# Two chunks of one layer a step in place of one chunk of each layer, in a four-layer convolution kernel

## Chip, cores, metric

The kernel runs on one core of a Trainium2 chip, as one program. The metric is device time in microseconds (us) of that core. The engines are TensorE (PE: matrix products; its weight loads are PEld), VectorE (DVE), ScalarE (ACT), GpSimd (POOL) and SyncE (SP, which here only issues DMA transfers).

## What is computed

The input `x` has 16 images of 64 channels of 128 x 128 values in float32. Four layers follow one another, each of the form "x plus a function of the group-normalized x":

```
x = x + L0(gn(x))     # 64x64 gram matrix of the image, applied to it, then a 1x1 product with conv_w
x = x + L1(gn(x))     # per channel two 3x3 gradient filters, |gx| + |gy|
x = x + L2(gn(x))     # a quarter of the channels shifted left, a quarter right, then 3x3 conv W, plus b
x = x + L3(gn(x))     # 3x3 conv w_bin, 1x1 conv w1x1, plus b1x1, batch norm over ALL images, leaky, clip(0, 255)
```

Every normalization needs sums over a whole image before the first value of the next layer can be made. The batch norm in layer 3 needs sums over all 16 images, so the last addition can only be made when layer 3's products of every image are done.

## The kernel before

An image is cut into `NS` = 8 chunks. Each image passes three stages: `Front` (layers 0 and 1, lines 557 to 703), `Layer2` (836 to 994) and `Layer3` (997 to 1086). After all images a tail reads back `x3` (the output of layer 2) and `y` (the convolution of layer 3) from DRAM, or makes `y` again for the six images in `AGAIN`, and writes the output (1334 to 1357).

The order of the work is written out by hand. The class `InOrder` (64 to 76) keeps every engine's instructions in the order in which the program issues them; it is also why the profile shows nearly everything at L74. The main loop (1176 to 1241) goes through steps, and each step has four quarters `q` = 0 to 3. `starts` (1091) says that the front begins at step 15, layer 2 at step 25 and layer 3 at step 35, each 8 steps later for the next image. So a step in the middle handles one chunk of `Front` of image b+2 or so, one chunk of `Layer2` of an earlier image and one chunk of `Layer3` of a still earlier one.

What the stages do in a step, with the names that the profile shows:

- `Front`: TensorE mixes the image with a 64 x 64 matrix (`po<-x,abd`; for images from `EARLY` = 3 on in four 64 x 64 tiles of the array, `mix_four`). ScalarE normalizes the result into `xh`. VectorE makes the two filters in eight instructions (`u`, `e`; method `sobel`, 664): two in quarter 0, four in quarter 1, one in quarter 2 (`u<-xh,co,u`) and one in quarter 3 (`u<-e,co,u`). Ahead of the last two ScalarE takes absolute values of `u` and `e` ("first of 2", 682). The result is stored to DRAM (`x_d<-u`), and ScalarE squares it for the statistics (`junk<-u`).
- `Layer2`: loads a chunk of the front's output (`v<-x_d`), ScalarE normalizes it (`v<-v,co`, `edges`, two single columns `v<-v,kc`, 931 to 949), VectorE makes a difference of neighbouring rows (`d2a`, `d2b`; method `different`, 873), and POOL copies these differences to the other half of the partitions (`q`). TensorE forms `one` (products that two output rows share) and `two` (those that they don't). ScalarE evicts `one` to `c`; VectorE adds `two` and `c` to `x` (908 to 921), and ScalarE squares that (`junk<-x`).
- `Layer3`: the same from tiles in SBUF, with `d` for the difference, and `y` for the sum (1065 to 1087).

Products that use only half of the rows of the array are issued in lists `straight` and `across`; `section` (747) runs them side by side in four quadrants of the array. In steps where both layers have a chunk, layer 3's go to `straight` and layer 2's, from the copy `q`, to `across`. In the other steps (`both_layers` is false, 741) the layers use packed weights (`packed`, 255) and copies of both kinds instead. PSUM has two buffers for `two` and one for `one`.

Before a layer can begin an image, the coefficients must be made: a chain of small instructions (`coefficients`, 300), given out link by link over following quarters by `tick`. TensorE sums (`bank<-st`), VectorE makes mean and variance (`me`, `nv`), POOL takes the power (`va`, `co`). The chains of the Gram matrix (`gram_chain`, 322) go the same way. The Gram products themselves (`bank<-xw`, 128 products of 64 x 65 for an image) lie in three steps of eight; ScalarE copies the rows of the image for them (`xw<-xr`). The first six images have their Gram at double pace (`2 * EARLY`).

All loads and stores of the main loop are issued by SP, except the copies `q` on POOL.

Of the kernel before, what the change touches and what calls it, by code (L numbers as in the profile page):

```python
# [16 lines left out]
P = 128  # L17
# [3 lines left out]
R = 8  # L21
NS = HH // R
EARLY = 3
# [87 lines left out]
def tile_kernel(ctx: ExitStack, tc: tile.TileContext, x, cw_h, w2_t, b2, wbin_t, w1_t, b1, gamma, beta, consts, out):  # L111
# [40 lines left out]
    def planes(d, shift=0):  # L152

        return d[W + shift:W + shift + 2 * C * PLANE].rearrange("(p j w) -> p j w", j=NP, w=W)
# [44 lines left out]
    wb = ring.tile([P, (R + 1) * W + 2], F32, tag="v2", name="wb", bufs=3)  # L199
    wb = wb[0:C, 0:9 * C].rearrange("p (y x c) -> p y x c", y=3, x=3)  # L200
    w1 = ring.tile([P, R + 2, W], F32, tag="v3", name="w1")[0:C, 0, 0:C]
# [23 lines left out]
    d2, q2, d3 = [], None, None  # L225
    for name in ("d2a", "d2b", "q2", "d3"):
        t = wpool.tile([P, 2, CP, W + 2], F32, name=name)
        pool.memset(t, 0.0)
        if name in ("d2a", "d2b"):
            d2.append(t)  # L230
        elif name == "q2":
            q2 = t
        else:
            d3 = t
# [12 lines left out]
    packed = {}  # L247
    cross = wpool.tile([P, 2, C], F32, name="cross")

    def other_weights():  # L250
        for n in range(2):
            o = 1 - single(TO_SLOTS, n)[0]
            pool.tensor_copy(wm[:, :, cols(o)], w2[:, n, :, cols(o)])

        for name, w, table in (("pk2", w2, TO_SLOTS), ("pk3", w3, TO_PAIRS)):
            dve.tensor_add(w[:, 2], w[:, 0], w[:, 1])
            packed[name] = wpool.tile([P, 2, C], F32, name=name)
            for n in range(2):
                o, i = single(table, n)
                for kx, half in ((1, i), (0, 1 - i)):  # L260
                    pool.tensor_copy(
                        packed[name][half * C:(half + 1) * C, n], w[i * C:(i + 1) * C, n, kx, o * C:(o + 1) * C]
                    )
        for n in range(2):
            o, i = single(TO_SLOTS, n)
            for kx in (1, 2):
                pool.tensor_copy(cross[cols(1 - i), kx - 1], w2[cols(i), n, kx, cols(o)])
# [31 lines left out]

    def coefficients(st, put, back=None):  # L300

        yield
        yield from when(TENSOR)
# [6 lines left out]
        yield from rstd(pm, r, me, GN_EPS, None if back is None else co[:, 2:3])  # L310
# [6 lines left out]
        put(co)  # L317

# [3 lines left out]
    def gram_chain(b, pg):  # L322
# [4 lines left out]
        if b > 2 * EARLY:  # L327
            dve.tensor_reduce(gs, pg.rearrange("p (j c) -> p c j", j=3), axis=AX.X, op=ALU.add)
        else:
            dve.tensor_copy(gs, pg)  # L330
        while b > 2 * EARLY and now[0] < NS * b - 4:
            yield
# [61 lines left out]
        abd = stp.tile([P, P], F32, tag="abd", name=f"abd_{b}", bufs=EARLY + 3)  # L394
# [37 lines left out]
        co = stp.tile([P, 5], F32, tag="co1", name=f"co1_{b}", bufs=EARLY + 3)  # L432
# [22 lines left out]
    def first_gram():  # L455
# [7 lines left out]
        for m in range(NS):  # L463
            t = ring.tile([P, 2, CP, W], F32, tag="x3", name=f"x_first_{m}", bufs=NS + 2)
            t = t.rearrange("p a j w -> p (a j w)")
            for h in range(2):
                sp.dma_start(t[h * C:(h + 1) * C], halves(x[0].rearrange("c h w -> (c h w)"), h, m * R, R))
            src.append(t)
        for m in range(NS + 1):
            if m < NS:  # L470
# [3 lines left out]
                for h, copy in ((0, dve.tensor_copy), (1, act.copy)):  # L474
                    copy(xw[:, m * R:(m + 1) * R, 0:C, h], two[:, :, h * C:(h + 1) * C])
# [14 lines left out]
    class Gram:  # L490
        first, last = 2, NS + 2
# [4 lines left out]
        def at(self, i, q):  # L496
# [7 lines left out]
            if i == 2 and q == 0:  # L504
                for m in range(3):
                    self.load(m)
            m = {11: 0, 13: 1, 15: 2, 19: 3, 21: 4, 23: 5, 27: 6, 31: 7}.get(4 * i + q)
# [5 lines left out]
        def part(self, n):  # L513
# [3 lines left out]
            if self.b <= 2 * EARLY:  # L517
# [17 lines left out]
        def half(self, r):  # L535
# [6 lines left out]
            if self.b > 1 and m is not None:  # L542
# [4 lines left out]
                elif self.b < 2 * EARLY:  # L547
                    live.setdefault((Gram, self.b + 1), Gram(self.b + 1)).load(m + 3 - NS)
# [8 lines left out]
    class Front:  # L557
# [14 lines left out]
        def load(self, i):  # L572
            b = self.b
            t = xin.tile([P, R, W], F32, tag="x", name=f"x_{b}_{i}")
            if self.four:
# [3 lines left out]
                for g in range(2):  # L579
                    j = (i * R + g * CP) * W  # L580
                    sp.dma_start(t[cols(g)].rearrange("p h r w -> p h (r w)"), v[:, :, j:j + CP * W])
            else:
                for h in range(2):
                    sp.dma_start(flat(t[h * C:(h + 1) * C]), halves(x[b].rearrange("c h w -> (c h w)"), h, i * R, R))
# [28 lines left out]
        def at(self, i, q):  # L613
            b = self.b
            if q == 0:
# [16 lines left out]
                if i == NS:  # L632
                    chains.append(coefficients(self.st, lambda co: coefs2.update({b: co}), b2_sb))
# [30 lines left out]
        def sobel(self, i, q):  # L664
# [12 lines left out]
            if q == 1:  # L677
                dve.scalar_tensor_tensor(h, h, 3.0, self.u[:, 1:R + 1, :], op0=ALU.mult, op1=ALU.add)
                dve.scalar_tensor_tensor(p, self.e[:, :, 1:W + 2], 3.0, p, op0=ALU.mult, op1=ALU.add)
                dve.tensor_sub(gx, h[:, :, 2:W + 2], gx)  # L680
# [14 lines left out]
        def store(self, i):  # L695
            d = planes(x2_d[self.b]).rearrange("(c s) j w -> c s j w", s=2)
            for h in range(2):
                for s in range(2):
                    j0 = (h * HH + i * R) // 2
                    sp.dma_start(  # L700
                        d[:, s, j0:j0 + R // 2, :],
                        self.x2[i][h * C:(h + 1) * C].rearrange("p (j s) w -> p s j w", s=2)[:, s],
                    )
# [19 lines left out]
    def taps(o, p, wts, srcs, pad=0):  # L723

        made = []
        for kx in (1, 0, 2):
            o0, o1 = (0, W) if kx == 1 else (1, W) if kx == 0 else (0, W - 1)
            for wt, src in zip(wts, srcs):
                made.append((
                    p[cols(o), :, o0:o1], wt[:, kx, cols(o)], src[:, :, o0 + kx - 1 + pad:o1 + kx - 1 + pad]  # L730
# [9 lines left out]

    def both_layers(step):

        return starts[0][1] <= step < starts[1][1] + NS * B
# [31 lines left out]
    def products(p, wts, srcs):  # L775
        issue([taps(o, p, wts, srcs) for o in range(2)])

    def shared(p, wt, t, m=CP):  # L780
        products(p[:, 0:m], [wt], [by_parity(t)[1][:, 0:m]])

    def own(p, n, table, wt, d, pk, q=None, m=CP, both=None):
        d = d[:, n, 0:m]
        o, _ = single(table, n)
        some = [[], []]
        some[1 - o] = taps(1 - o, p[:, 0:m], [wt[:, n] if both is None else both], [d], 1)
        if q is not None:
            some[o] = [
                (p[cols(o), 0:m], pk[:, n], q[:, n, 0:m, 1:1 + W]),  # L790
                (p[cols(o), 0:m, 0:W - 1], wt[:, n, 2, cols(o)], d[:, :, 2:1 + W]),
            ]
        issue(some)

    def apart(two, table, wt, d):

        for kx in range(3):
            for n in range(2):
                o, i = single(table, n)
                straight.append((  # L800
                    two[cols(o), n], wt[cols(i), n, kx, cols(o)], d[cols(i), n, :, kx:kx + W], kx == 0, kx == 2,
                ))

    def apart_across(two, table, q, m):

        for kx in range(3):
            for n in range(2):
                o, i = single(table, n)
                w = W - 1 if kx == 2 else W
                wt = cross[cols(1 - i), kx - 1] if kx else packed["pk2"][cols(1 - i), n]  # L810
                across.append((
                    two[cols(o), n, 0:m, 0:w], wt, q[cols(1 - i), n, 0:m, kx + 1:kx + 1 + w], kx == 0, kx == 2,
                ))
# [22 lines left out]
    class Layer2:  # L836
        first, last = -2, NS

        def __init__(self, b):
            self.b, self.v, self.whole, self.edges, self.p = b, {}, {}, {}, {}  # L840
# [3 lines left out]
        def load(self, i):  # L844
# [4 lines left out]
            t = ring.tile([P, N], F32, tag="v2", name=f"v2_{b}_{i}", bufs=3)  # L849
            for c0, c1, shift in ((0, C // 4, 1), (C // 4, C // 2, -1), (C // 2, C, 0)):  # L850
                cut = R * W + 1 - shift
                parts = [(0, i * R, N)] if i + 1 < NS else [(0, i * R, cut), (cut, -R, N)]
                for at, j, end in parts:
                    for s in range(2):

                        first = j * W + at - 1 + shift
                        src = x2_d[b][W + first:W + first + 2 * C * PLANE].rearrange("(c s n) -> s c n", s=2, n=PLANE)
                        sp.dma_start(t[s * C + c0:s * C + c1, at:end], src[s, c0:c1, 0:end - at])
# [14 lines left out]
        def different(self, i):  # L873

            d, t = d2[i % 2], self.v[i]
            even, odd, _ = by_parity(t)
            difference(d, spread(even, 2 * W), odd, CP if i + 1 < NS else CP - 1)
            for n in range(2):
                _, k = single(TO_SLOTS, n)
                if not both_layers(now[0] + 1):  # L880
                    pool.dma_start(flat(q2[cols(k), n]), flat(d[cols(k), n]))
                pool.dma_start(
                    flat(q2[cols(1 - k), n])[:, 1:CP * (W + 2)], flat(d[cols(k), n])[:, 0:CP * (W + 2) - 1]
                )
# [17 lines left out]
        def at(self, i, q):  # L902
            b = self.b
            closing = i + 1 == NS
            m = CP - 1 if closing else CP
            if q == 0:
                if i == NS:
                    chains.append(coefficients(self.st, self.done))
                if 1 <= i:
                    two = self.p.pop(i - 1)[0]  # L910

                    e = self.edges.pop(i - 1).rearrange("p t (m n) -> p n m t", n=2)
                    ends = two[:, :, :, 0:W:W - 1]
                    dve.tensor_add(ends, ends, e)
                    x3 = ring.tile([P, 2, CP, W], F32, tag="x3", name=f"x3_{b}_{i - 1}", bufs=NS + 2)
                    tiles3[b].append(x3)
                    dve.scalar_tensor_tensor(
                        x3.rearrange("p s j w -> p s (j w)"), two.rearrange("p s j w -> p s (j w)"), 1.0,
                        self.c.unsqueeze(1).to_broadcast([P, 2, CP * W]),
# [476 lines left out]
```

## Time and profile before

Three runs took 2579.61 us in the median (2579.11 to 2585.26). The profiled execution took 2579.28 us, of which its span is 2577.4 us. Its mean granted TensorE clock is 0.974.

| what | value |
|---|---|
| VectorE's first filter instruction of step 15, 24, 25, 35 (start) | 45.22, 145.76, 159.97, 308.57 us |
| the same, step 106, 114 | 1415.89, 1539.73 us |
| the same, step 129, 137, 142 (last) | 1761.87, 1878.66, 1952.19 us |
| last product of layer 3's `two` ends | 2170.7 us |
| DMA in the tail, 2250 to 2450 us | 416 to 417 GB/s |
| DMA over the span | 235 GB/s |
| a copy `q` on POOL: issue, to landing | 0.53 us, 3.0 to 3.3 us |

The start of VectorE's instruction `u<-xh 128x1170` marks a step of the front; there are 128 of them, steps 15 to 142. In a timeline the first number is the start, the second the duration; engines overlap the end of an instruction with the beginning of the next, so what an instruction costs its queue is the distance of two starts. [...]

### The profile page before, as it was taken

Reading aid. Unit: us, or ns where it says so; the run is one execution under the profiler, and the core shown is the slowest. Engines: PE = TensorE matmul, PEld = TensorE weight load, DVE = VectorE, ACT = ScalarE, POOL = GpSimd, SP = SyncE. Lnnn points to the kernel's source line nnn. Section 1 sums busy time; section 2 is a strip of 40 time slices with the busy share of each in tenths; the row PEclk is TensorE's granted clock in tenths of the full one; section 3 lists DMA queues with packets and bytes.
Section 4 is the critical chain, followed back from the end, with each engine's and each line's share of the span. In section 5 each row is a group of like instructions: output and inputs, shape, how many; then the busy total and the mean of one; then the engine's idle time right before and its main releaser. Section 6 shows DMA issues by size and latency. Waiting matters only on the chain.

```text
span 2577.4 us, 52786 instructions
## 1 busy us (share of the span) xinstructions
PE 2436.5 (95%) x19206; PEld 958.9 (37%) x19206; DVE 2091.8 (81%) x2811; ACT 2137.0 (83%) x3549; POOL 504.3 (20%) x805
## 2 busy tenths in 40 slices
PE   6568899999999999999999999999999998999995
PEld 4334343434343434343434343333333333333342
DVE  4998889999999999999999999999997334443433
ACT  4778879898989898989898988888987568877775
POOL 3332312011121212111112121202111100222222
PEclk8778999999999999999999999999999999999998
DMA  8789969898877777777777777778787767999998
GB/s 207 202 230 237 242 171 254 207 251 208 238 188 206 181 199 190 198 190 194 195 182 199 205 188 193 199 201 211 201 201 178 190 197 251 405 417 417 417 413 334
DMA packets 624979, 605.00 MB, mean 235 GB/s; under 512 B 53536, under 2 KB 525504, under 8 KB 624720
## 3 DMA queue, kind: packets, MB, share of 16 engines
q1 hardware_dynamic: 591696, 496.76, 70.0%
q0 software_dynamic: 33024, 104.87, 12.2%
q8 instruction: 153, 2.51, 0.4%
q14 instruction: 106, 0.87, 0.1%
HBM read 321.46 MB, written 243.28 MB: 219 GB/s over the span
## 4 chain that ended last, share of the span: by engine, by line
PE 46%; DMA 20%; DVE 15%; ACT 7%; SPq 7%; issue 4%; POOL 1%; DVEq 0%; POOLq 0%; ACTq 0%
PE two L74 22%; PE one L74 15%; SPq L74 7%; DVE u L74 5%; DMA end_x<-x_d 4%; PE bank L74 3%; DVE e L74 3%; PE po L74 2%; DMA x_d<-u 2%; PE two_again L74 2%; DMA x<-in_x 2%; DMA xw<-x_d 2%; ACT v L74 2%; DVE d L74 2%; DVE y L74 2%
## 5 line engine op out<-in xcount | busy, mean ns | idle before, releaser
L74 PE MATMUL two<-d,w 64*64 64x512 f32 (+2 forms) x2992 | 692.5, 593 | 0.0
L74 PE MATMUL two_again<-v_again,w 64*64 64x508 f32 (+1 forms) x3456 | 374.0, 590 | 10.6 <-ACT v_again L74 10.6
L74 PE MATMUL one<-v,w 128*64 128x508 f32 (+2 forms) x1600 | 362.1, 584 | 7.3 <-ACT c L74 6.9
L74 PEld LDWEIGHTS two<-d,w 64*64 64x64 f32 (+1 forms) x2992 | 206.6, 134 | 418.4 <-issue 408.3
L74 PE MATMUL one<-v,wi 128*64 128x508 f32 (+3 forms) x1536 | 353.7, 595 | 0.0
L74 DVE SCALAR_TENSOR_TENSOR e<-e 128x1032 f32<-128x1032 f32 (+1 forms) x256 | 313.4, 1224 | 0.0
L74 ACT ACTIVATE xh<-po,co 128x128 f32<-128x128 f32 (+1 forms) x480 | 274.7, 622 | 26.7 <-PE po L74 21.4
L74 PE MATMUL po<-x,abd 64*64 64x512 f32 (+1 forms) x1024 | 184.4, 617 | 52.9 <-ACT xh L74 49.7
L74 DVE SCALAR_TENSOR_TENSOR y<-two,c 128x1024 f32<-128x1024 f32 x128 | 156.2, 1220 | 95.1 <-ACT v L74 65.5
L74 PEld LDWEIGHTS two_again<-v_again,w 64*64 64x64 f32 x3456 | 138.4, 134 | 245.4 <-issue 214.4
L74 PE MATMUL two<-q,cross 64*64 64x508 f32 (+3 forms) x944 | 215.9, 573 | 0.0
L74 POOL DMA_DIRECT2D q<-d2b x138 | 72.2, 527 | 721.0 <-DVE d2b L74 417.7
L74 ACT ACTIVATE v<-x,co 128x1024 f32<-128x1024 f32 (+3 forms) x256 | 203.8, 846 | 0.0
L74 POOL DMA_DIRECT2D q<-d2a x138 | 73.8, 537 | 646.3 <-issue 312.7
L74 DVE TENSOR_TENSOR d<-v 128x1024 f32<-128x1024 f32 x128 | 156.3, 1221 | 47.0 <-ACT v L74 29.2
L74 PEld LDWEIGHTS one<-v,w 128*64 128x64 f32 x1600 | 110.9, 137 | 204.2 <-issue 162.9
L74 ACT ACTIVATE v<-v,co 128x1154 f32<-128x1154 f32 x128 | 172.1, 1344 | 14.0 <-DMA v<-x_d 10.4
L74 PE MATMUL two<-d2a,wi 128*64 128x508 f32 (+1 forms) x768 | 183.2, 589 | 0.0
L74 DVE SCALAR_TENSOR_TENSOR u<-xh 128x1170 f32<-128x1170 f32 x128 | 175.9, 1374 | 5.2 <-ACT xh L74 4.4
L74 DVE SCALAR_TENSOR_TENSOR u<-xh,co,u 128x1024 f32<-128x1024 f32 x128 | 163.9, 1280 | 14.6 <-ACT u L74 14.6
L74 PE MATMUL two<-d2b,wi 128*64 128x508 f32 (+3 forms) x768 | 174.3, 565 | 0.0
L74 PEld LDWEIGHTS one<-v,wi 128*64 128x64 f32 x1536 | 101.2, 138 | 193.9 <-issue 156.1
(231 smaller groups left out, 4323.6 us busy)
## 6 DMA issues: line engine op xcount, KB each, us to landing
x<-in_x SPq DMA_DIRECT2D x256, 256.0 KB
x_d<-u SPq DMA_DIRECT2D x512, 128.0 KB
x_d<-x SPq DMA_DIRECT2D x490, 128.0 KB
xr<-in_x SPq DMA_DIRECT2D x120, 512.0 KB
y_d<-y SPq DMA_DIRECT2D x320, 128.0 KB
v<-x_d SPq DMA_DIRECT2D x448, 72.1 KB
v<-x_d SPq DMA_DIRECT2D x224, 144.2 KB
end_x<-x_d SPq DMA_DIRECT2D x39, 512.0 KB
```

The lines of the kernel that those rows point to most:

```text
L74: return self.tc.keep_in_program_order(call(*args, **kwargs))
```

## The change

The stages `Layer2` and `Layer3` are called by a plan instead of by fixed starts. A step takes two chunks of one layer of one image. `start_of(b)` is 24 + 8 b; image b has its layer 2 in the steps `start_of(b)` to +3 and three of its four pairs of layer 3 in +5 to +7; the last pair follows at +12 (for the last image at +8), which is +4 of the next image.

```diff
-    starts = ((Layer3, 35), (Layer2, 25), (Front, 15))
+FIRST, LAG = 15, 9
+    def start_of(b):
+        return FIRST + LAG + NS * b
+    plan = {}
+    for b in range(B):
+        for p in range(NS // 2):
+            plan[start_of(b) + p] = Layer2, b, p
+            plan[start_of(b) + (5 + p if p < 3 or b + 1 == B else 12)] = Layer3, b, p
```

The even chunk's half-row products go to `straight`, the odd chunk's to `across`. For layer 2 the odd chunk reads the copy `q2`, so POOL copies the differences of odd chunks only. For layer 3 the odd chunk changes the halves of its output instead (`swap`). The packed weights and the copies for them go. Differences lie in `dA` (even) and two buffers `dB` (odd); layers share one ring of four tiles `v` and one of two tiles `c`.

The body of a step, after the change (stages have methods in place of one `at`):

```python
        before, here, after = (planned(step + d) for d in (-1, 0, 1))
        late = after[1] == 0
        for q in range(4):
            ...
            if q == 0:
                if stage and i == 0:
                    stage.different(1)
                if late:
                    finish()
                sobel("first of 0")
                if not late:
                    finish()
                if after[0] and not late:
                    after[0].norm(after[1])
                if stage:
                    stage.sums(i)
                    stage.one(i)
            if q == 1 and stage:
                stage.rest(i)
                stage.evict(i)
            if q == 1 and after[0] and not late:
                after[0].norm(after[1] + 1)
            if q == 1:
                quick_product()
            if q == 2:
                sobel("first of 2")
                if stage:
                    stage.one(i + 1)
            if q == 3 and stage:
                stage.rest(i + 1)
                stage.evict(i + 1)
            for b in fronts:
                run(Front, b, step - FIRST - NS * b, q)
            if q == 0 and late:
                after[0].load(0)
            if q == 0 and before[0]:
                before[0].square(before[1] + 1)
                if before[1] + 2 == NS:
                    before[0].close()
            if q == 1:
                quick_rest()
                if stage:
                    stage.sums(i + 1)
                    for j in range(2):
                        stage.apart_of(i + j)
                if before[0]:
                    before[0].store(before[1] + 1)
            section()
            if q in (1, 3):
                stage2, j = planned(step + 2)
                if stage2 and j + q // 2:
                    stage2.load(j + q // 2)
            if q == 2:
                if stage:
                    stage.combine(i)
                if late:
                    after[0].norm(0)
                elif after[0]:
                    after[0].different(after[1])
            if q == 3:
                if late:
                    after[0].norm(1)
                    after[0].mixed_weights()
                    after[0].different(0)
                elif after[0]:
                    after[0].different(after[1] + 1)
                if stage:
                    stage.square(i)
                    stage.store(i)
```

`finish` combines the odd chunk of the step before (`before[0].combine(before[1] + 1)`). A step is `late` if the next one begins an image in its layer. `combine` is VectorE's sum `x<-two,c` or `y<-two,c`, `norm` ScalarE's normalization, `evict` ScalarE's `c<-one`, `different` VectorE's difference (and POOL's `q`). The coefficients of layers 2 and 3 are no longer spread over quarters: the product is in quarter 1 and the rest is put between the second and the third filter instruction of that quarter:

```diff
             if q == 1:
                 dve.scalar_tensor_tensor(h, h, 3.0, self.u[:, 1:R + 1, :], op0=ALU.mult, op1=ALU.add)
                 dve.scalar_tensor_tensor(p, self.e[:, :, 1:W + 2], 3.0, p, op0=ALU.mult, op1=ALU.add)
+                quick_rest()
                 dve.tensor_sub(gx, h[:, :, 2:W + 2], gx)
```

Loads of `x` and `v` are shared by SP and POOL, and the image between front and layer 2 lies in DRAM in halves, so that a chunk is stored by two transfers of 128 partitions:

```diff
-                    sp.dma_start(t[cols(g)].rearrange("p h r w -> p h (r w)"), v[:, :, j:j + CP * W])
+                    (sp, pool)[g].dma_start(t[cols(g)].rearrange("p h r w -> p h (r w)"), v[:, :, j:j + CP * W])
...
-                        sp.dma_start(t[s * C + c0:s * C + c1, at:end], src[s, c0:c1, 0:end - at])
+                        (sp, pool)[s].dma_start(t[s * C + c0:s * C + c1, at:end], src[s, c0:c1, 0:end - at])
```

Smaller parts: `EARLY` is 2, and the Gram is at double pace for images 1 to 3 only (`FAST` = 3):

```diff
-EARLY = 3
+EARLY, FAST = 2, 3
-        pace[b] = at, 2 if b <= 2 * EARLY else 1
-        at += NS // pace[b][1] + (1 if b == 2 * EARLY else 0)
+        pace[b] = at, 2 if b <= FAST else 1
+        at += NS // pace[b][1] + (2 if b == FAST else 0)
-            m = {11: 0, 13: 1, 15: 2, 19: 3, 21: 4, 23: 5, 27: 6, 31: 7}.get(4 * i + q)
+            m = {9: 0, 11: 1, 13: 2, 15: 3, 17: 4, 19: 5, 21: 6, 23: 7}.get(4 * i + q)
```

The last table places ScalarE's row copies for the Gram, which now lie in the steps +4 to +7 of an image. The first image is loaded in eight transfers of 128 partitions in place of sixteen of 64. The list of buffers that the tail reads into follows the new tiles.

## Prediction

> **What bounds the kernel now.** A "step" is one turn of the main loop; it has four quarters, 0 to 3. "Both layers" are layers 2 and 3. I read the page's first two parts, then busy time in stretches, then the order of work on VectorE and ScalarE inside one step.
>
> ```profile
> PE 2436.5 (95%) x19206; PEld 958.9 (37%) x19206; DVE 2091.8 (81%) x2811; ACT 2137.0 (83%) x3549; POOL 504.3 (20%) x805
> PE   6568899999999999999999999999999998999995
> DVE  4998889999999999999999999999997334443433
> PEclk8778999999999999999999999999999999999998
> ```
>
> TensorE is busy from slice 7 on, and VectorE with it until slice 30. Only the first six slices and the last few have TensorE room. Stretches of 50 us (columns: busy of PE, weight loads, DVE, ACT, POOL, then granted clock, DMA share, GB/s):
>
> ```profile
> 150.00:200.00 50.00, 34.95 (x275) 14.53 (x272) 44.57 (x70) 42.39 (x71) 15.12 (x22) 0.86 0.84 230
> 250.00:300.00 50.00, 43.83 (x462) 22.38 (x460) 39.93 (x66) 36.64 (x62) 20.93 (x29) 0.89 0.91 240
> 1300.00:1350.00 50.00, 49.10 (x358) 17.46 (x356) 49.26 (x66) 47.02 (x81) 7.00 (x12) 1.00 0.70 181
> 2150.00:2200.00 50.00, 43.64 (x300) 15.97 (x300) 24.32 (x41) 42.73 (x60) 7.32 (x14) 1.00 0.78 266
> ```
>
> In the middle TensorE, VectorE and ScalarE all have under 3 us of 50 to spare: nothing there can wait without the end moving. VectorE inside a step (start us, us):
>
> ```profile
> 1306.47 1.37 DVE L74 SCALAR_TENSOR_TENSOR u<-xh 128x1170 f32<-128x1170 f32 x1
> ...
> 1313.78 1.22 DVE L74 SCALAR_TENSOR_TENSOR e<-e 128x1024 f32<-128x1024 f32 x1
> 1314.92 1.22 DVE L74 SCALAR_TENSOR_TENSOR y<-two,c 128x1024 f32<-128x1024 f32 x1
> 1316.06 0.08 DVE L74 DVE_READ_ACCUMULATOR y<-two,c 128x1 f32 x1
> 1316.06 1.22 DVE L74 TENSOR_TENSOR d<-v 128x1024 f32<-128x1024 f32 x1
> 1317.20 1.22 DVE L74 TENSOR_TENSOR d2b<-v 128x1024 f32<-128x1024 f32 x1
> 1318.33 1.28 DVE L74 SCALAR_TENSOR_TENSOR u<-xh,co,u 128x1024 f32<-128x1024 f32 x1
> ```
>
> and ScalarE in the same step:
>
> ```profile
> 1311.79 1.40 ACT L74 ACTIVATE v<-v,co 128x1154 f32<-128x1154 f32 x1
> 1313.22 1.26 ACT L74 ACTIVATE edges<-v,co 64x8 f32<-64x8 f32 x4
> 1314.52 0.51 ACT L74 ACTIVATE v<-v,kc 128x9 f32<-128x9 f32 x2
> 1314.93 1.04 ACT L74 ACTIVATE u<-u 128x1024 f32<-128x1024 f32 x1
> 1315.88 1.04 ACT L74 ACTIVATE e<-e 128x1024 f32<-128x1024 f32 x1
> 1316.83 1.04 ACT L74 ACTIVATE junk<-x 128x1024 bf16<-128x1024 f32 x1
> ```
>
> The reader is to see the cover. ScalarE's absolute value of `u` ends at 1315.97; VectorE uses it at 1318.33, because `y`, `d` and `d2b` (3.4 us) lie between. ScalarE squares `x` after the absolute values, so its wait for VectorE's `x<-two,c` delays nothing. VectorE's steps are then 14.47 us apart (1292.00, 1306.47, 1320.94), which is its own work. With Gram products on TensorE three steps in eight are 16.4 us (1350.97, 1367.37, 1383.84, 1400.24). Eight steps, one image, take 123.84 us with Gram (1415.89 to 1539.73) and 116.79 without (1761.87 to 1878.66).
>
> **The change part by part.** *Fewer steps.* Before, layer 3 ran 20 steps behind the front, so steps 13 to 163 ran: 151. After, 13 to 153: 141. Work is conserved, so what is won is idle TensorE at both ends. Before, VectorE starts step 24 at 145.76 and TensorE's last layer 3 product ends at 2170.7; the span ends 406.7 later, and 1.9 us lie around it (2579.28 against 2577.4; the median of the runs, 2579.61, is the same). After, with periods as they are: 145.8 to step 24; eight steps, of image 0 alone, at 15 (those of before with one chunk took 11 to 19): 120; then 14 images, 12 with Gram (images 4 to 15 at single pace) and two without: 12 x 123.84 + 2 x 116.79 = 1719.7; then steps 144 to 152 without a front, 13.14 each (products `one<-v,wi` at 2052.11, 2065.26, 2078.40): 118.3; the tail, bound by 417 GB/s of transfers of unchanged size, 406.7; and 1.9. Sum 2512. The solo form of products (7.16 us a step, 2134.51 to 2141.67, against 13.14/2 = 6.57) goes too, and is in this sum.
>
> *Order on VectorE and ScalarE.* This is the dear part. In the new loop VectorE does `u<-xh,co,u` first in quarter 2, and `combine` and `different` after it: the 3.4 us of cover are gone. And ScalarE now has, ahead of the absolute values, the square of the chunk that VectorE combined in quarter 0, an eviction `c` and a normalization. That closes a ring. In a step that prepares layer 2: square 1.04, `c` 0.57 (1304.98 to 1305.55), layer 2's normalization with edges 3.14 (1311.79 to 1314.93), absolute value 1.04: 5.8 us on ScalarE. Then VectorE: `u` 1.20, combine with edges 1.44 (1308.91 to 1310.35), difference 1.14, last `u` 1.21, difference 1.14, next `u`,`e` 2.44, combine 1.44, and ScalarE's next square waits for that: 10.0. Ring 15.8 us, where VectorE's own work is 14.47. For layer 3 the normalization is 1.52 and a Gram row copy of 1.08 comes in: 14.7.
>
> *The turn to layer 2.* The first pair of layer 2 is normalized in quarters 2 and 3 of the step before, after its coefficients, while ScalarE must also normalize the next pair at quarters 0 and 1: four times 3.14 between two absolute values. From one to the next: 4 x 3.14, two absolute values 1.90, `xh<-po` twice 2.02, `c` twice 1.14, squares 3 x 1.04, row copy 1.08: 21.8. The coefficients add a wait for POOL: from VectorE's `nv` to `co` POOL took 4.0 us (1258.64 to 1262.59), and ScalarE has 3 to 4 us of other work; 0 to 2, I take 0.6, since the VectorE half is put early in quarter 1. So 22.4. Queued behind the second normalization: `different(1)`, first on VectorE in the next step, and behind it POOL's copy `q` (issue 0.53, 3.0 to landing), for which TensorE's section waits; I see TensorE idle some 3 us twice there.
>
> *The turn to layer 3.* Its normalizations are half as long and lie in a Gram step of 16.4, which hides them; without Gram that step is some 17.
>
> So an image, absolute value to absolute value: turn 22.4, two layer 2 steps 31.6, three Gram steps 49.2 as before (TensorE bounds them), 14.7, and 14.6 (VectorE's own): 132.5, against 123.84. Without Gram the three steps are 14.5 + 14.5 + 17 = 46: 129.3, against 116.79. Over 14 images 12 x 8.7 + 2 x 12.5 = 129. In the first eight steps the same turn adds about 7. That is 136 lost and 67 won (2579.3 - 2512): 2512 + 129 + 7 = 2648, and the late start of layer 2 at step 144 without a front 3: about 2650.
>
> *Queues.* Half of the `x` loads, half of the `v` loads go from SP to POOL; stores of the front are two of 128 partitions in place of four. SP issues 2115 transfers in place of 2891, POOL 926 in place of 466 (its 276 copies `q` become 128). 460 x 0.53 = 244 us over 2577 on an engine 20% busy: it hides, except where a load stands ahead of coefficients on POOL, at the turn 3 x 0.53 = 1.6 us, in the bound above. If loads ahead of it wait for buffers, another 2 us a turn, 30 in all. A gain from SP: ScalarE waited for a load of `v` twice in the whole run, 10.4 us together; I take 0, at most 10. [...] *Mixing of image 2 by four* (`EARLY` 2) takes 8 x 0.86 = 7 us off TensorE in steps that VectorE bounds: 0. The Gram of images 4 to 6 goes from double to single pace: the same products, two more of them in the middle, 2 x 7, counted above as Gram images.
>
> [...] The turn opens gaps of about 3. The rows are of both kinds: 43.83 of 50 busy had clock 0.89, but 43.64 of 50, with one gap of 2.88 us, had 1.00. [...] I take 0 and let the range have the rest.
>
> **The rivals.** *Filling wins.* One mechanism: idle ends of the pipeline are closed, and VectorE's and ScalarE's lateness at the turns is worked off in the three Gram steps, where each has 16.4 - 14.47 = 1.9 us of room, so that TensorE never stops. For it: TensorE sets those steps now. Against: only two `two` buffers let TensorE run ahead, and rings of 15.8 lie outside Gram steps. It gives 2512, or up to 2571 with half of the loss. It decides from the point where an image grows by less than 67/14 = 4.8 us. [...] *The change does nothing.* TensorE bound all through, and the last 20 steps hidden behind prefetch of the tail: 2579. Against: the tail starts only after layer 3's statistics.
>
> **How the numbers follow.** Rings as worked out, 2605 to 2690: 0.55. Rings partly absorbed, 2571 to 2605: 0.12, on the slower side nearly all. Filling wins: 0.20. Worse: 0.12. Nothing: 0.01. The predicted time is 2650. To leave out 2 in 10, the range goes from 2545 (a part of filling) to 2720. About 0.3%, or 8 us, is what a measurement can tell from no change: faster 0.20, same 0.04, slower 0.76.
>
> **What would show it.** Right: distances of `u<-xh 128x1170` on VectorE that alternate, near 22 at the turn to layer 2 and near 15.8 in the two steps after; VectorE idle before `u<-xh,co,u` with ACT `u` as releaser, hundreds of us in place of 14.6; TensorE under 95% busy in the middle; an image of about 132 us; last layer 3 product near 2240. Wrong: images of 124 to 127 us, or steps 16.4 where I have 22. If Gram steps grow beyond 17, the clock or the loads on POOL are what I have missed.

## The result: 2785.0 us, and the profile after

The changed kernel took 2785.04 us in the median of four runs (2780.54 to 2788.44), beside 2579.36 us for the kernel before on the same chip: ratio 1.0798 [1.0784, 1.0812], 206 us slower. 2650 had been predicted, in a range that ended at 2720. Its profiled execution has a span of 2786.6 us.

The page after, the same rows as shown of before:

```profile
PE 2523.0 (91%) x19286; PEld 978.1 (35%) x19286; DVE 2099.1 (75%) x2811; ACT 2120.4 (76%) x3509; POOL 714.3 (26%) x1254
PE   6598999999898989898989898989898999999996
DVE  5999888888778888888888878887998933444333
PEclk8599999999999999999999999999999999999998
```

VectorE and ScalarE are busy for as long as before within 1%, in a longer span. TensorE now has an 8 in about every second slice of the middle, where all were 9. The ends did fill: TensorE was busy for 34.95 us of the stretch from 150 to 200 us before, and for all 50 now, while the clock there went from 0.86 to 1.00:

```profile
150.00:200.00 50.00, 50.00 (x362) 18.76 (x360) 47.01 (x72) 42.42 (x83) 19.64 (x33) 1.00 0.66 175
```

One image with Gram, cut into eight steps at the starts of `u<-xh 128x1170` (columns: busy of PE, weight loads, DVE, ACT, POOL, then granted clock, DMA share, GB/s). The steps are +6 and +7 of the image before, then +0 to +5 of an image; layer 2 is in +0 to +3, its first chunks are normalized in +7, and Gram products lie in +2, +3 and +4:

```profile
1101.71:1118.59 16.88, 15.41 (x90) 4.91 (x88) 16.03 (x21) 14.63 (x24) 3.24 (x6) 1.00 0.78 195
1118.59:1137.37 18.78, 15.91 (x106) 5.51 (x104) 15.84 (x27) 13.69 (x27) 9.90 (x18) 1.00 0.63 152
1137.37:1156.27 18.90, 16.27 (x88) 5.58 (x86) 15.17 (x24) 18.38 (x37) 5.86 (x9) 1.00 0.46 111
1156.27:1172.17 15.90, 11.54 (x54) 4.61 (x50) 14.42 (x18) 10.14 (x19) 4.96 (x10) 0.79 0.60 170
1172.17:1190.13 17.96, 17.96 (x176) 7.97 (x174) 14.17 (x19) 15.48 (x31) 4.51 (x9) 1.00 0.67 186
1190.13:1210.07 19.94, 19.94 (x218) 10.96 (x216) 15.84 (x22) 14.19 (x26) 2.43 (x5) 1.00 0.97 235
1210.07:1229.03 18.96, 17.99 (x180) 7.79 (x178) 13.58 (x19) 10.56 (x16) 4.21 (x8) 1.00 0.35 100
1229.03:1245.22 16.19, 16.19 (x94) 5.26 (x92) 15.29 (x28) 15.99 (x23) 2.59 (x3) 1.00 0.41 121
```

In the first four rows TensorE stands (1.5, 2.9, 2.6 and 4.4 us) and once runs at clock 0.79. In the next two it is never idle: what was not made earlier is made there. A whole image, first before, then after:

```profile
1044.22:1168.09 123.87, 122.98 (x986) 47.82 (x984) 119.71 (x166) 112.38 (x196) 23.51 (x37) 1.00 0.76 193
```

```profile
1101.71:1245.22 143.51, 131.22 (x986) 52.58 (x984) 120.33 (x165) 113.06 (x196) 37.70 (x67) 0.98 0.61 159
```

The same 986 records of products. An image is 19.6 us longer: TensorE is idle 12.3 us in place of 0.9, and busy 8.2 us longer with the same products; part of that is the clock, which was 0.50 for 6.8 us of this image (1160.9 to 1167.7). POOL's 14 us more go with its issues of loads (39 of them in this image, some 20 us, where it issues 8 copies `q` fewer).

Where VectorE and ScalarE wait, in the table of waits of after (us in total, times, longest us):

```profile
DVE u L75 <- ACT u L75: 187.8, 94, 4.8
DVE two L75 <- PE two L75: 95.8, 26, 15.2
ACT xw L75 <- PE bank L75: 90.5, 11, 8.2
PE two L75 <- DMA q<-dB: 68.5, 27, 5.4
DVE dB L75 <- ACT v L75: 40.9, 28, 2.5
```

The first row was foretold (14.6 before). The second (21.0 before), TensorE's lateness as VectorE meets it, and the third, the row copies for the Gram that wait for Gram products, were not. The fourth was foretold in kind and size (27 waits of 2.5 us in the mean, where some 3 us twice a turn were expected), but the sum gave it no cost.

Three places in the image show where the first, third and fourth rows come from. *The row copy*, on ScalarE in step +4, and what follows it there:

```profile
1220.19 1.16 ACT L75 COPY xw<-xr 128x1024 f32<-128x1024 f32 x1 [8.22 <-PE bank L75]
1221.24 1.05 ACT L75 ACTIVATE u<-u 128x1024 f32<-128x1024 f32 x1
```

The new table of row copies puts the first copy for the next image into the quarter in which the last Gram products of this image are made. They read `xw`, the copy overwrites it, and in ScalarE's queue the absolute value that VectorE needs stands behind it; VectorE then waits 4.83 us for that.

*The copy `q`*, on POOL between steps +0 and +1, and TensorE's products from it:

```profile
1154.66 1.96 POOL L75 TENSOR_TENSOR co<-va,kc 128x1 f32<-128x1 f32 x2
1156.58 0.57 POOL L75 DMA_DIRECT2D v<-x_d  x1
1158.60 0.99 POOL L75 DMA_DIRECT2D v<-x_d  x2 [1.45 <-issue]
1159.58 1.04 POOL L75 DMA_DIRECT2D q<-dB  x2
```

```profile
1162.49 1.47 PE L75 MATMUL two<-q,cross 64*64 64x512 f32 x2 [4.36 <-DMA q<-dB]
1163.37 1.45 PE L75 MATMUL two<-q,cross 64*64 64x512 f32 x2
```

`dB` was made by 1155.6, but `q` is issued behind coefficients and three loads, at 1159.58. TensorE stands 4.36 us. The clock falls to 0.50 at 1160.9, still in this gap, and stays there to 1167.7.

*The missing cover*, on VectorE in step +0, as foretold (the cover is the work that VectorE had between ScalarE's absolute value of `u` and its own use of it):

```profile
1144.83 1.22 DVE L75 SCALAR_TENSOR_TENSOR e<-e 128x1024 f32<-128x1024 f32 x1
1149.22 1.29 DVE L75 SCALAR_TENSOR_TENSOR u<-xh,co,u 128x1024 f32<-128x1024 f32 x1 [3.17 <-ACT u L75]
```

### The profile page after: what moved, and what is told of

Same layout as the page of the kernel before. It is cut to its first block, busy times and chain, and to the rows that moved or that the text cites. A ratio compares the mean times of both kernels' runs of the same rounds, so it can differ in the third digit from the quotient of the medians.

```text
span 2786.6 us, 52813 instructions
## 1 busy us (share of the span) xinstructions
PE 2523.0 (91%) x19286; PEld 978.1 (35%) x19286; DVE 2099.1 (75%) x2811; ACT 2120.4 (76%) x3509; POOL 714.3 (26%) x1254
## 4 chain that ended last, share of the span: by engine, by line
PE 44%; DVE 19%; DMA 17%; ACT 11%; issue 6%; POOL 2%; SPq 1%; DVEq 0%; POOLq 0%; ACTq 0%
PE two L75 19%; PE one L75 11%; DVE u L75 7%; PE two_again L75 6%; PE bank L75 4%; ACT v L75 3%; DVE e L75 3%; DMA xw<-x_d 3%; DMA q<-dB 3%; DMA v<-x_d 3%; PE po L75 2%; DVE y L75 2%; DVE dA L75 2%; ACT u L75 2%; DVE dB L75 1%
## 5 line engine op out<-in xcount | busy, mean ns | idle before, releaser
L75 PE MATMUL two<-dA,w 64*64 64x512 f32 (+2 forms) x2304 | 569.9, 623 | 0.0
L75 PE MATMUL two<-dB,w 64*64 64x512 f32 (+2 forms) x1536 | 353.4, 593 | 8.7 <-DVE y L75 8.7
L75 POOL DMA_DIRECT2D v<-x_d x480 | 237.4, 501 | 390.4 <-PE one L75 188.2
L75 PE MATMUL two<-q,cross 64*64 64x512 f32 (+1 forms) x768 | 227.5, 675 | 89.0 <-DMA q<-dB 68.5
L75 DVE SCALAR_TENSOR_TENSOR u<-xh,co,u 128x1024 f32<-128x1024 f32 x128 | 164.5, 1285 | 187.9 <-ACT u L75 187.8
L75 PE MATMUL po<-x,abd 64*64 64x512 f32 (+1 forms) x1024 | 225.1, 646 | 32.6 <-ACT xh L75 29.2
L75 PEld LDWEIGHTS two<-dA,w 64*64 64x64 f32 (+1 forms) x2304 | 150.8, 138 | 251.2 <-issue 244.5
L75 ACT COPY xw<-xr 128x1024 f32<-128x1024 f32 x120 | 140.6, 1177 | 99.5 <-PE bank L75 90.5
L75 ACT ACTIVATE u<-u 128x1024 f32<-128x1024 f32 x128 | 134.5, 1051 | 100.5 <-DVE u L75 99.8
L75 DVE TENSOR_TENSOR dB<-v 128x1024 f32<-128x1024 f32 (+1 forms) x128 | 152.2, 1189 | 50.6 <-ACT v L75 40.9
L75 ACT ACTIVATE junk<-x 128x1024 bf16<-128x1024 f32 x128 | 134.8, 1053 | 72.4 <-DVE x L75 71.0
L75 ACT ACTIVATE c<-one,co 128x512 f32<-128x512 f32 x128 | 86.6, 677 | 123.9 <-PE one L75 123.8
```

What stands on the lines that cost most here:

```text
L75: return self.tc.keep_in_program_order(call(*args, **kwargs))
```

## Experiments

All times are medians beside the kernel before on the same chip (2577.9 to 2579.8). There are three theories of what costs the time: A, the row copy that waits for Gram products; B, the `q` copy behind loads on POOL, with or without the clock; C, the missing cover of `u<-xh,co,u`. "The turn" is the place where a new image begins layer 2, steps +7 and +0. Steps are told of the image shown above, by VectorE's starts.

**The row copy one quarter later.** From the changed kernel:

```diff
-            m = {9: 0, 11: 1, 13: 2, 15: 3, ...
+            m = {10: 0, 11: 1, 13: 2, 15: 3, ...
```

> The changed kernel (2785 us), only the first row copy of a Gram moved one quarter later, behind the last Gram products of the image before, which read the buffer that it overwrites. Theory A (the copy, waiting 8.2 us for TensorE in ScalarE's queue, holds up the absolute value and so VectorE in the last Gram step): that step goes from 18.96 us to TensorE's 16.4, so 12 x 2.6 = 31 us less, at most 12 x 4.8 = 58: 2727 to 2754. Rival (TensorE bounds Gram steps, the wait is hidden): 2780 to 2788.

Measured 2751.42 (2748.91 to 2754.91), ratio 1.067 [1.0653, 1.0688]: 33.6 us less. Step +4 went from 18.96 to 16.08 us, and the wait of `xw` for `bank` is gone from the table of waits. A holds: 2.8 us an image, 12 images.

**Loads of `v` all by SP.** From the changed kernel; the loads of `x` stay shared:

```diff
-                        (sp, pool)[s].dma_start(t[s * C + c0:s * C + c1, at:end], ...
+                        sp.dma_start(t[s * C + c0:s * C + c1, at:end], ...
```

> The changed kernel, only the loads of v back to SP alone. Theory B (on POOL these loads stand ahead of the copies q; TensorE then waits 4.4 us in the second step of layer 2 and comes back at half clock for some 5 us): the copy is issued some 3 us earlier, the gap falls under 2 us, the clock stays 1.00 there, 3 to 6 us an image less: 2700 to 2745. Rival (SP's own queue is now later by as much, or TensorE's gap is not on the path): 2775 to 2795.

Measured 2760.82 (2758.64 to 2763.63), ratio 1.0706 [1.0689, 1.0724]: 24.2 us less, the direction of B but less than it foretold. TensorE's waits for `q` fell from 68.5 to 32.6 us. Step +1 of the same image:

```profile
1152.67:1168.54 15.87, 15.87 (x86) 5.40 (x84) 14.42 (x18) 13.85 (x27) 2.01 (x4) 1.00 0.74 202
```

The step itself is as long as before (15.90), with clock 1.00 in place of 0.79. What got shorter is the step behind it, +2, from 17.96 to 15.60. Over the whole run the mean granted clock rose from 0.961 only to 0.967.

**The cover given back.** From the changed kernel, the instruction `u<-xh,co,u` goes behind `combine` and `different` of quarter 2:

```diff
-            if 0 <= i < NS:
+            if 0 <= i < NS and q != 2:
                 self.sobel(i, q)
...
                 elif after[0]:
                     after[0].different(after[1])
+                sobel(2)
```

> The changed kernel, only VectorE's instruction that uses the absolute value put behind combine and difference in quarter 2, as in the kernel before. Theory C (the ring absolute value, u, combine, square, eviction, normalization is longer than VectorE's work): VectorE's waits for ACT u fall from 188 us to under 60, the second layer 2 step from 15.9 to about 14.5, in all 14 x 3 to 14 x 6 = 40 to 85 us less: 2700 to 2745. Rival (the wait goes to another place, since ScalarE's queue is what is late): 2765 to 2790.

Measured 2712.34 (2710.96 to 2720.86), ratio 1.0516 [1.0498, 1.0534]: 72.7 us less, within C. VectorE's waits for ScalarE's `u` fell from 187.8 to 48.8 us. The step in which C looked for it was wrong: +1 did not fall to 14.5 but grew from 15.90 to 18.60, and +3 from 19.94 to 21.92; +0 (18.90 to 16.44), +2 (17.96 to 14.57) and the layer 3 steps +5 and +6 (0.9 each) fell, by more in all.

**The three edits together.**

> All three edits together. If the three causes are separate and these are all beside the turn to layer 2: 2785 - 31 - 50 - 60 = about 2645, between 2580 and 2690. If they cover one another (each wait hides the next): no better than the best of the three by more than 20 us.

Measured 2646.63 (2645.07 to 2651.24), ratio 1.0266 [1.0248, 1.0284]: 138.4 us less, where the three alone sum to 130.5: none of them hides another. The image takes 133.78 us.

**The same row copy in the kernel before.**

```diff
-            m = {11: 0, 13: 1, 15: 2, ...
+            m = {9: 0, 13: 1, 15: 2, ...
```

> The kernel before, only the first row copy of a Gram moved two quarters earlier, to where the change puts it: the same wait for TensorE now stands in ScalarE's queue there too. Theory C (what makes such a wait dear is that VectorE has no work between its filter instructions and the absolute value): here 3.4 us of sums and differences lie between, and the Gram step is bound by TensorE, so at most 9 x 1 us: 2578 to 2590. Rival (the wait is dear wherever it stands, 33.6/12 = 2.8 us each): 9 x 2.8 = 25 us more, 2603 or above.

Measured 2589.87 (2587.76 to 2592.96), ratio 1.0036 [1.0022, 1.005]: 10.1 us more, over nine images at this pace 1.1 us each. The same placing cost 2.8 us an image in the changed kernel. The number is that of theory C, but the trace does not show C's reason. In one image:

```profile
1019.50 1.16 ACT L74 COPY xw<-xr 128x1024 f32<-128x1024 f32 x1 [3.64 <-PE bank L74]
1021.63 1.29 DVE L74 SCALAR_TENSOR_TENSOR u<-xh,co,u 128x1024 f32<-128x1024 f32 x1 [2.44 <-ACT u L74]
```

The copy waits 3.64 us here, not 8.22, and VectorE waits in spite of its cover. Its step grows from 16.45 to 18.97 us, nearly as much as in the changed kernel (16.08 to 18.96); but the step behind it falls from 16.38 to 14.93, where the changed kernel's stayed at 16.19. The wait was cheaper because the next step made up for it. Whether the cover had a part in that is not shown.

**The turn: VectorE's order.** From the kernel of three edits; the filter's first two instructions go ahead of the difference that waits, and `finish` behind both:

```diff
             if q == 0:
+                sobel("first of 0")
                 if stage and i == 0:
                     stage.different(1)
-                if late:
-                    finish()
-                sobel("first of 0")
-                if not late:
-                    finish()
+                finish()
```

> The three edits (2647 us), and at the turns VectorE begins with the next filter instructions u and e: difference(1) and the last sum of the image before come after them. In the trace of the three edits VectorE waits 2.4 us for the second normalization at each turn to layer 2, 2.1 at the turn to layer 3 and 3.3 for TensorE's last products; u and e are 2.4 us of work that can lie there. If these waits are on the path: 14 x 4 to 14 x 6.5 = 56 to 90 us less, 2557 to 2590. If the turn is bound by ScalarE's four normalizations and by the copy q (TensorE's gap of 3.0 us and half clock after it): under 20 us less, 2627 or above.

Measured 2626.99 (2622.59 to 2632.56), ratio 1.0184 [1.0168, 1.02]: 19.6 us less, not the 56 or more of my theory; the rival held (under 20).

**The turn: ScalarE's order.** From the kernel just told; the second normalization goes behind the absolute values:

```diff
-            if q == 1 and after[0] and not late:
-                after[0].norm(after[1] + 1)
...
             if q == 2:
                 sobel("first of 2")
+                if after[0] and not late:
+                    after[0].norm(after[1] + 1)
```

> As e6, and ScalarE takes the absolute values ahead of a step's second normalization. If ScalarE's row of normalizations bounds the turn: 3.1 us less for each image, 14 x 3 = 43 us below e6. If e6 already took the waits away, or the difference of the odd chunk now waits for that normalization: e6 within 15 us, on either side.

Measured 2615.1 (2610.99 to 2615.72), ratio 1.0133 [1.012, 1.0147]: 11.9 us less, where my theory had 43; the rival held (within 15).

**Row copies closer together**, also from the kernel with VectorE's new order:

```diff
-            m = {10: 0, 11: 1, 13: 2, 15: 3, 17: 4, 19: 5, 21: 6, 23: 7}.get(4 * i + q)
+            m = {10: 0, 11: 1, 13: 2, 15: 3, 17: 4, 18: 5, 20: 6, 21: 7}.get(4 * i + q)
```

> As e6, and the last three row copies of a Gram one to three quarters earlier, so that none lies between the normalizations of the turn to layer 2. A row copy costs ScalarE 1.08 us in the chain of the turn: at most 14 x 1.1 = 15 us below e6 if that chain is the bound; within 4 us of e6 if it is not.

Measured 2621.4 (2614.04 to 2622.02), ratio 1.0155 [1.014, 1.017]: 5.6 us less, between the theory (up to 15) and the rival (within 4), and hardly clear of the runs' spread.

**Both of these.**

> The last two edits that helped, together: the turn's second normalization moved behind the absolute values (11.9 us when added alone) and the closer spacing of the row copies (5.6 us alone). If they are separate costs, 2615.1 - 5.6 = 2609.5, within 2603 to 2615. If both only freed the same time of ScalarE, no change from 2615.1.

Measured 2609.7 (2605.99 to 2615.86), ratio 1.0123 [1.01, 1.0146], as the sum said. It is the fastest of the new orders, and still 30 us behind the kernel before. One image of it, and the step of its turn:

```profile
1039.59:1171.04 131.45, 125.95 (x988) 49.61 (x986) 120.41 (x164) 113.75 (x196) 24.33 (x36) 0.99 0.65 174
```

```profile
1055.85:1075.62 19.77, 16.08 (x82) 5.43 (x80) 16.39 (x24) 17.75 (x38) 4.49 (x6) 0.91 0.47 119
```

**Other products into the turn's gap.** From that kernel: `po<-x,abd` ahead of the products that wait for `q`, in the first step of a layer's image.

```diff
+    def mixes():
+        for dst, wt, src, start, stop in mixed:
+            pe.matmul(dst, wt, src, start=start, stop=stop)
...
+            if q == 1 and stage and i == 0:
+                mixes()
             section()
```

> As the run before it in this call, with the eight mixing products po<-x,abd (1.9 us) of the turn step issued ahead of the products that wait for the copy q, instead of behind them. In the trace of the kernel before this edit TensorE stood 3.46 us at this place, and the products behind it ran at half clock (2.0 and 1.75 us records in place of 1.1), clock 0.92 in a step of 20.83 us. Theory: TensorE's gap and its clock bind the turn; the gap falls to about 1.6 us, the clock there to 1.00, together 1.9 + 1.6 = 3.5 us a turn, 14 turns: about 49 us, 2550 to 2575, which would be level with or below the kernel before. Rival: ScalarE, busy 19.67 of the 20.83 us, binds the turn by its four normalizations; then at most 15 us, 2595 to 2612.

(The 3.46 us, clock 0.92 and 20.83 us in it are of the kernel with ScalarE's new order but without the closer row copies; the kernel of both, from which the edit was made, has 3.69, 0.91 and 19.77 at this place.)

Measured 2632.31 (2630.42 to 2634.76), ratio 1.0211 [1.0191, 1.0232]: 22.6 us *slower*; neither theory had that. TensorE's own row of waits for `q` left the list (26.8 us in the kernel without the edit), and another grew, from 27.4 us to this:

```profile
PE po L75 <- ACT xh L75: 56.0, 27, 5.4
```

The mixing products need the room that ScalarE's `xh` copies free, and those stand behind its normalizations. So TensorE waits at the turn in this order too, and the step of the turn has clock 0.92 in the image looked at. The edit acts at the turn to layer 3 as well, where step +5 grew from 17.20 to 18.07 us.

**The turn's second difference first again**, on top:

```diff
+                if stage and i == 0:
+                    stage.different(1)
                 sobel("first of 0")
-                if stage and i == 0:
-                    stage.different(1)
                 finish()
```

> As the run before it in this call, but VectorE makes the turn's second difference dB ahead of the front's two first filter instructions again, so that the copy q starts about 2.5 us earlier. Theory of the gap: the rest of the gap (about 1.6 us) closes, 10 to 20 us less than the run before. Rival: dB then waits some 2 us for ScalarE's second normalization and everything on VectorE stands behind it; no gain, or up to 20 us slower.

Measured 2647.71 (2645.93 to 2649.08), ratio 1.0268 [1.025, 1.0285]: 15.4 us slower again. The rival held: VectorE waited 67.2 us for ScalarE's `v` in `dB`.

**Only the clock.** From the changed kernel; one product that is made anyway is made six more times in the gap ahead of the products that wait for `q`, in layer 2's second step:

```diff
+            if q == 1 and isinstance(stage, Layer2) and i == 2:
+                dst, wt, src, start, stop = straight[0]
+                for n in range(6):
+                    pe.matmul(dst, wt, src, start=True, stop=True)
+                last[0] = 1
             section()
```

> The changed kernel, with six idle products in the gap before the products that wait for the copy q in layer 2's second step: the first of these products (two<-dA,w, 0.53 us each) is made six times over, about 3.2 us of a gap of 4.36 us; each writes what the next overwrites, so the result is not touched. Nothing else is changed: the copy q lands when it did. Theory of the clock: the granted clock was 0.50 from 1162 to 1166 us after the gap and 0.56 up to 1168; with the gap filled it stays at 1.00, the sixteen products (1.45 us records in place of 0.7) end some 2.7 us sooner, and as ScalarE's and VectorE's next instructions waited for them, 16 images: 2785 - 43 = 2742, within 2730 to 2760. Rival: the lateness comes from the wait for q alone, and the ring between ScalarE and VectorE hides TensorE's slower products; then within 10 us of 2785.

Measured 2765.1 (2761.59 to 2769.86), ratio 1.0732 [1.0709, 1.0754]: 19.9 us less by doing more. The size was half of what I had expected (43 us, from 16 images); the rival's "within 10" is out. The mean granted clock rose from 0.961 to 0.977. Steps +1 and +2 of the image:

```profile
1154.38:1170.26 15.88, 15.88 (x78) 5.87 (x74) 14.43 (x19) 12.45 (x22) 7.43 (x16) 1.00 0.67 188
1170.26:1185.86 15.60, 15.60 (x164) 6.75 (x162) 14.15 (x19) 13.16 (x29) 2.04 (x4) 1.00 0.71 195
```

Loads and copies were on POOL as in the changed kernel, and yet +2 is 15.60, just as with the loads taken off POOL. So in this image the whole gain of that run can be had through the clock, without an earlier landing.

## Why the prediction was wrong in size

The sum went from one absolute value on ScalarE to the next. These are those of after:

```profile
1126.20 1.06 ACT L75 ACTIVATE u<-u 128x1024 f32<-128x1024 f32 x1 [4.64 <-DVE u L75]
1148.15 1.04 ACT L75 ACTIVATE u<-u 128x1024 f32<-128x1024 f32 x1
1165.06 1.04 ACT L75 ACTIVATE u<-u 128x1024 f32<-128x1024 f32 x1
1183.27 1.05 ACT L75 ACTIVATE u<-u 128x1024 f32<-128x1024 f32 x1
1197.88 1.05 ACT L75 ACTIVATE u<-u 128x1024 f32<-128x1024 f32 x1
1221.24 1.05 ACT L75 ACTIVATE u<-u 128x1024 f32<-128x1024 f32 x1
1237.48 1.05 ACT L75 ACTIVATE u<-u 128x1024 f32<-128x1024 f32 x1
1253.18 1.06 ACT L75 ACTIVATE u<-u 128x1024 f32<-128x1024 f32 x1
```

With the one before them (1109.68) their distances answer the terms of the sum:

| term | predicted | measured |
|---|---|---|
| turn to layer 2 (+7 to +0) | 22.4 | 21.95 |
| two layer 2 steps (+0 to +2) | 31.6 | 16.91 + 18.21 = 35.1 |
| three Gram steps (+2 to +5) | 49.2 | 14.61 + 23.36 + 16.24 = 54.2 |
| layer 3, +5 to +6 | 14.7 | 15.7 |
| layer 3, +6 to +7 | 14.6 | 16.5 |
| an image | 132.5 | 143.5 |

11.0 us an image over 12 images with Gram are 132 of the 135 us that were missing. The rest of the sum held: the filled ends (step 32 starts at 273.68, where 145.8 + 127 = 272.8 was predicted), the images without Gram (128.4 and 129.2 for 129.3) and the turn. By VectorE's starts, which the prediction had named as the sign, no step was near 22: the turn lies in two steps of 18.8 and 18.9.

*The step that failed is "three Gram steps 49.2 as before (TensorE bounds them)"*: 5.0 of the 11.0 us. It took these steps as if their length came from their own work. Two things were not in it. First, the new table of row copies: the copy's own 1.08 us were counted, but no wait, and one copy now waits 8.22 us for Gram products, with the absolute values behind it. That is 33.6 us, by the run with one number changed. A step that is moved must be held against what its buffer's readers are doing then. Second, "TensorE bounds them" means that they have no room: what TensorE did not make at the turn and in +1 is made there. This was seen when filling the gap in +1 left +1 as it was and cut +2. The prediction's own sign of this, Gram steps over 17, came true (17.96, 19.94 and 18.96 by VectorE's starts); it pointed to the clock and to the loads on POOL, and not to the row copy.

*Two smaller terms failed with it.* The two layer 2 steps were 3.5 us longer, of which 2.3 are the clock: with the gap filled, 18.21 became 15.87, the ring's 15.8. The last two terms were 2.9 us longer; the 14.6 among them stood as "VectorE's own" work, but with the cover given back 15.70 and 16.53 became 14.81 and 15.61, so that the missing cover was paid there too.

*The clock* was taken at 0 by the row of 43.64 us in 50, and the range and the chance of "Worse" were to hold what it might cost; no run shows the price that they counted it at. That row was misread: it has not one gap of 2.88 us but two, of 2.88 and 3.42 us (shown at the end). The gap in +1 came out at 4.36 us and the clock at 0.50 for 6.8 us; the run with the gap filled puts it at 19.9 us in all. Shorter gaps did not all leave the clock alike (see the last section).

*POOL's queue* was taken at 0 to 30 us for loads ahead of others. `q` does stand behind loads (1159.58 instead of about 1156.6), and taking the loads of `v` off POOL gave 24.2 us. In the image shown the clock alone gives as much. Over the run it need not be so: the mean granted clock rose by 0.006 with these loads moved, but by 0.016 with the gap filled, for a like gain. How the 24.2 us divide is open. A load of `v` of 64 KB landed 0.8 to 1.1 us later by POOL than by SP (medians 3.4, and 2.3 to 2.6 us).

*The cover* was named rightly, with 14.6 us of wait turned into 187.8; giving it back alone won 72.7 us, part of which the prediction had charged as the ring.

*Rival "filling wins"* needed an image to grow by less than 4.8 us (its "2571 with half of the loss" should read 2512 + 68 = 2580; nothing rests on it). The point can be tested at the best order, the run of both edits. From step 32 on its 12 images with Gram take 130.6 us in the mean, 6.7 more than before, and the two without 121.4 and some 119.0, 4.6 and 2.2 more: 87 us. The steps ahead of them, those without a front and the tail add 7; less 67 of filling, 27 are left, and the two profiled executions differ by 28. So the gain of the filled ends is there, and is lost again in the images. What is left shows at the turn, and the clock is the smaller part of it. In the image shown the clock was 0.91 in one step, and the image took 131.45 us. But four later images ran at clock 1.00 throughout:

```profile
1318.94:1836.26 517.32, 500.28 (x3940) 195.06 (x3938) 481.24 (x654) 445.73 (x773) 92.71 (x140) 1.00 0.74 197
```

That is 129.3 us an image, still 5.5 more than before, with TensorE idle 4.3 us in place of 0.9, most of it at the turn (in the third of the four, gaps of 1.25 and 1.88 us). Three orders of that place moved the wait from `q` to `xh` and to `v`, all of which come from ScalarE, and none removed it. That its four normalizations of 3.1 us in a row are the reason agrees with all three, but no run took one of them away, so it is not shown. Of the 132 us, 34 are the row copy and 20 the clock; that these two add up was not run. For the others (some 78) only the places are known, not a price for each.

## What to carry to other kernels

When a change moves work between steps, add up the bound engine's idle and slow time over a whole period; do not take each step's length as the larger of its own parts, since an engine that is full in the later steps pays there for earlier stops. For each instruction that moves, look up who still reads its destination, and what stands behind it in its queue: here one number in a table was worth 34 us. This case also suggests, though no run parted it from the rest, that two layers with a chunk each in a step give an engine something else to do while one waits, where two chunks of one layer need the same producer at the same time.

## What the runs showed of the hardware

Six products whose results are overwritten, put into a gap of 4.36 us, made the kernel 19.9 us faster, as the clock stayed at 1.00 in the image shown. What a shorter gap does is not as plain. With the mixing products put first, the turn of one image had two gaps, of 1.25 and 1.85 us, in place of 1.25 and 3.69, and the clock still fell (columns as above, two us each):

```profile
1070.00:1072.00 2.00, 0.56 (x6) 0.28 (x7) 2.00 (x3) 2.00 (x5) 0.00 (x0) 1.00 1.03 229
1072.00:1074.00 2.00, 2.00 (x14) 0.71 (x12) 1.69 (x2) 1.97 (x5) 0.00 (x0) 0.70 1.05 182
1074.00:1076.00 2.00, 2.00 (x12) 0.78 (x9) 0.00 (x0) 2.00 (x4) 0.00 (x0) 0.50 0.39 97
1076.00:1078.00 2.00, 2.00 (x16) 0.59 (x10) 1.05 (x2) 1.94 (x5) 0.00 (x0) 0.95 0.00 0
```

In the kernel before, two longer gaps, of 2.88 and 3.42 us, left it at 1.00 (the mean of the row from 2150 to 2200 us that the prediction shows):

```profile
2173.62 0.61 PE L74 MATMUL bank<-mv,kc 128*128 128x2 f32 x4 [2.88 <-DVE mv L74]
2188.06 12.17 PE L74 MATMUL two_again<-v_again,w 64*64 64x512 f32 x112 [3.42 <-ACT v_again L74]
```

So in these traces the length of one gap does not decide whether the clock falls. What does is not shown.
